# One transposed form of the tokens in the first phase, router logits put together from extra matmul columns, and a gathered copy of each sequence's columns

## The chip, the cores and the metric

The kernel runs on one core of one Trainium2 chip. The core has five engines that work side by side, each through its own instructions in program order: TensorE (PE in the profile; its weight loads are shown apart as PEld), VectorE (DVE), ScalarE (ACT), GpSimd (POOL) and SyncE (SP), which here only issues DMAs. An engine that must wait for another one's result stands still, and everything behind the waiting instruction in its own queue stands with it. The metric is the device time of one execution in microseconds (us). Three runs of the kernel before took 988.33, 989.93 and 993.07 us; the median is 989.93 us.

## What is computed

The input is 32 "rows" s of 256 positions b with 128 features. It is normalised, and the result xn goes into two blocks; the output is x plus both.

```python
xn = _layernorm(x, axis=-1)
x = x + _L0_attn_ref(xn, ...) + _L0_ffn_ref(xn, ...)
```

The first block (`_L0_attn_ref`) is an attention over the 256 positions of each of the 32 rows, 16 heads of 8 features; its scores are a covariance of q and k plus a product of their variances. In the kernel this is the second phase, and a "sequence" there is one s with its 256 positions.

The second block (`_L0_ffn_ref`) is an ordinary transformer layer whose sequence runs the other way: over the 32 values of s at one position b. It normalises xn again (weights ln1), projects to q, k, v, does causal attention of 32 x 32 with 16 heads, projects out, adds the input (x1), normalises x1 (weights ln2), computes eight router logits, and sends each token to its two best experts:

```python
hn = layernorm(x, ln1_w, ln1_b);  qkv = hn @ in_proj_w.T + in_proj_b
...
x1 = x + attn @ out_proj_w.T + out_proj_b
hn2 = layernorm(x1, ln2_w, ln2_b)
logits = hn2 @ router_w.T
```

In the kernel the attention and the router inputs are the first phase; the routing and the experts run inside the second phase.

## The kernel before

**First phase.** The 8192 tokens are cut into 16 chunks (`NCHUNK`) of 512, four tiles k of 128 tokens; a tile holds four positions c of 32 tokens each. `first_rounds` is a software pipeline of rounds i = -2 to 15. Round i works on several chunks at once: it loads chunk i+5, normalises i+3 (`norms`), measures i+4 (`measure`), transposes i+2 (`turn_in`), projects i+2 to k, q and v (`project_in`), spreads the v of i+1 through DRAM (`spread`), computes the scores of i+1, takes the softmax of i and i+1 in four groups g (`lessened` on DVE, `exponents` on ACT, `turn_weights` on PE and ACT), weighs v for i and i-1 (`weigh`, `divide`), and projects out, adds and measures i-1 (`turn_out`, `project_out`). Behind these come `normalise` of i-1 (GpSimd) and `turn_normed` and `logits` of i-2. The order of the calls in the round is written out by hand, and it is the order in which every engine meets its instructions.

Two transposed forms of the tokens are made there: `turn_in` transposes xn (L305, into `xnT`, kept for the second phase) and the twice normalised tokens zn (L310, into `hT`, with ln1's weight and bias applied on the way out of PSUM). `turn_normed` (L442) makes a third, ln2's result, which is used for the router alone (L448).

**PSUM.** The eight PSUM banks are two pools of four, `bank_u` and `bank_w`. A tile takes the bank of its pool that was released longest ago. So if tiles of one pool are used up in the order in which they are made, a tile takes the bank of the tile made four places before it, and waits until that one has been read for the last time. In one round of before, `bank_u` hands out, in this order: pta, ptb, po (second half), ptp0, ptp1, pto, pq, pv, ptp2, ptp3, ptc, po (first half), pl.

**Second phase.** 32 sequences, two units u each; `step(t)` makes score blocks (`sm` and their transposes `sT`), takes maxima on DVE (L622), exponentials on ACT (L625), and weighs (L634). `project` (L557) multiplies a sequence's transposed tokens, read straight out of `xnT` with a step of 32 elements, by Wq, Wk, Wv. `route` is a generator whose steps are dealt out between the units, four a unit up to t = 96 and eight a unit after; its first 49 steps work out the routing and the next 128 scatter the tokens to DRAM (L801). The experts follow in the middle of the phase. `last_rounds` deals out the end of the first phase between the first seven steps of the second.

Of the kernel before, what the change touches and what calls it, by code (L numbers as in the profile page):

```python
# [68 lines left out]
def block_kernel(  # L69
# [26 lines left out]
    xv = x.rearrange("s (i c k) e -> i c s (k e)", c=4, k=4)  # L96
# [7 lines left out]
    xnT = cp.tile([P, NCHUNK, 512], F32, name="xnT")  # L104
# [14 lines left out]
    rv = resd.rearrange("s (i c k) e -> i c s (k e)", c=4, k=4)  # L119

    vec = cp.tile([P, 7], F32, name="vec")
    l1w, l1b, l2w, l2b = (vec[:, n:n + 1] for n in range(4))
# [5 lines left out]
    mhalf = cp.tile([P, 4, 1], F32, name="mhalf")  # L128
    wqkv = cp.tile([P, 3, P], F32, name="wqkv")
    wo = cp.tile([P, P], F32, name="wo")  # L130
    inT = cp.tile([P, 3, P], F32, name="inT")
    outT = cp.tile([P, P], F32, name="outT")
    rT = cp.tile([P, NE], F32, name="rT")

# [5 lines left out]
    def load(i):  # L140
        xt = ax.tile([P, 4, P], F32, tag="xt", name=f"xt{i}")
        for c in range(4):
            nc.sync.dma_start(xt[32 * c:32 * c + 32].rearrange("s k e -> s (k e)"), xv[i, c])
        return xt
# [13 lines left out]
    late = xnT[:, NCHUNK - 2:NCHUNK].rearrange("p i t -> p (i t)").rearrange("p (n m) -> p n m", m=P)  # L158
    ipw, opw, qkw, rw, bvs = late[:, 0:3], late[:, 3], late[:, 4:6], late[0:NE, 6], late[:, 7]
    qkT, ccen = zx[:, NTILE - 2:NTILE], zx[:, NTILE - 3]  # L160

    def loads():
# [7 lines left out]
        nc.scalar.dma_start(opw, out_proj_w)  # L170
        nc.scalar.dma_start(bout, out_proj_b.partition_broadcast(P))
# [3 lines left out]
        nc.sync.dma_start(rw, router_w)  # L175
# [5 lines left out]
    def set_in():  # L181
        nc.vector.tensor_scalar(bk4, cst[:, C_M4:C_M4 + 4], bk, None, ALU.mult)
        pt = bank_u([P, 4, P], "pt0")
        for n in range(3):
            nc.tensor.transpose(pt[:, n, :], ipw[:, n, :], ident)
        nc.tensor.transpose(pt[:, 3, :], opw, ident)
        nc.vector.tensor_copy(inT[:, 0:2, :], pt[:, 0:2, :])

        nc.vector.tensor_copy(
            inT[:, 2, :].rearrange("p (j g d) -> p j g d", j=4, g=4),  # L190
            pt[:, 2, :].rearrange("p (g j d) -> p j g d", j=4, g=4),
        )
        nc.vector.tensor_copy(outT, pt[:, 3, :])


        nc.vector.tensor_copy(bvs, bv.to_broadcast([P, P]))
        pbo = bank_u([P, P], "pbo")
        nc.tensor.matmul(pbo, bvs, outT, start=True, stop=True)
        nc.vector.tensor_tensor(bout, bout, pbo, ALU.add)

    def set_rest():
        pt = bank_w([P, 4, P], "pt1")
        nc.tensor.transpose(pt[:, 0, :], qkw[:, 0, :], ident)
        nc.tensor.transpose(pt[:, 1, :], qkw[:, 1, :], ident)
        nc.tensor.transpose(pt[:, 2, 0:NE], rw, ident[0:NE, 0:NE])
        nc.vector.tensor_copy(qkT, pt[:, 0:2, :])
        nc.vector.tensor_copy(rT, pt[:, 2, 0:NE])
# [3 lines left out]
        nc.vector.tensor_copy(wqkv[:, 0:2, :], pb)  # L211

# [42 lines left out]
    xts, rss, nrm, mvs, zns, hTs, qTs, kbt, scs, prs, pTs, wps, os, oTs, x1s, h2s = ({} for _ in range(16))  # L255

    def stats(src, tag, i, bufs=2):

        st = a2.tile([P, 4, 6], F32, tag="st", name=f"st{tag}{i}")
        mv = a2.tile([P, 4, 2], F32, tag=f"mv{tag}", name=f"mv{tag}{i}")  # L260
# [3 lines left out]
        rs = a2.tile([P, 4, 1], F32, tag=f"rs{tag}", name=f"rs{tag}{i}")  # L264
# [4 lines left out]
    def measure(i):  # L269
# [10 lines left out]
        nc.gpsimd.tensor_tensor(r2, r2, mhalf, ALU.pow)  # L280
        nrm[i] = rs, nb, r2

# [20 lines left out]
    def turn_in(i):  # L303

        nc.scalar.copy(  # L305
            xnT[:, i, :].rearrange("p (c k s) -> p k c s", c=4, k=4),
            transposed(tokens(i), "a", i).rearrange("p (k c s) -> p k c s", k=4, c=4),
        )
        hTs[i] = a2.tile([P, 512], F32, tag="hT", name=f"hT{i}")
        nc.scalar.activation(hTs[i], transposed(zns.pop(i), "b", i), AF.Identity, bias=l1b, scale=l1w)  # L310
        nc.gpsimd.tensor_tensor(tokens(i), tokens(i), bout.unsqueeze(1).to_broadcast([P, 4, P]), ALU.add)

    def project_in(i):
        hT = hTs.pop(i)
        pk = bank_w([P, 512], f"pk{i}")
        nc.tensor.matmul(pk, inT[:, 1, :], hT, start=True, stop=True)  # L316
# [5 lines left out]
        nc.tensor.matmul(pq, inT[:, 0, :], hT, start=True, stop=True)  # L322
        qTs[i] = a2.tile([P, 512], F32, tag="qT", name=f"qT{i}")
        nc.scalar.activation(qTs[i], pq, AF.Identity, bias=bq, scale=1.0)
        pv = bank_u([P, 4, 4, 32], f"pv{i}")
        for k in range(4):
            nc.tensor.matmul(pv[:, :, k, :], hT[:, k * P:(k + 1) * P], inT[:, 2, :], start=True, stop=True)
        nc.scalar.copy(
            vs[i % 2].rearrange("p j k g d -> p (j k g) d")[:, :, 0:HD],
            pv.rearrange("p j k (g d) -> p (j k g) d", d=HD),  # L330
        )
        nc.sync.dma_start(vald[i], vs[i % 2].rearrange("p j k g d -> p j (k g d)"))
# [86 lines left out]
    def project_out(i):  # L419

        oT = oTs.pop(i)
        px = bank_w([P, 4, P], f"px{i}")
        for k in range(4):
            nc.tensor.matmul(px[:, k, :], oT[:, k * P:(k + 1) * P], outT, start=True, stop=True)  # L424
        x1 = x1s[i] = a2.tile([P, 4, P], F32, tag="x1", name=f"x1{i}")
        nc.vector.tensor_tensor(x1, px, tokens(i), ALU.add)
# [3 lines left out]
        for c in range(4):  # L430
            nc.sync.dma_start(rv[i, c], xt[32 * c:32 * c + 32].rearrange("s k e -> s (k e)"))

    def normalise(i, eng=nc.gpsimd):
        x1, mv, rs = x1s.pop(i), mvs.pop(i), rss.pop(i)
        for k in range(4):
# [4 lines left out]
    def turn_normed(i):  # L440
        h2s[i] = a2.tile([P, 512], F32, tag="h2", name=f"h2{i}")
        nc.scalar.activation(h2s[i], transposed(tokens(i), "c", i), AF.Identity, bias=l2b, scale=l2w)  # L442

    def logits(i):
        pl = bank_u([P, 4, NE], f"pl{i}")
        h2 = h2s.pop(i)
        for k in range(4):
            nc.tensor.matmul(pl[:, k, :], h2[:, k * P:(k + 1) * P], rT, start=True, stop=True)  # L448
        nc.vector.tensor_copy(lg[:, 4 * i:4 * i + 4, :], pl)
# [4 lines left out]
    def first_rounds():  # L454
# [6 lines left out]
        set_in()  # L461
        measure(1)
        set_values(0)
        for i in range(-2, NCHUNK):
# [23 lines left out]
            if i == NCHUNK - 1:  # L488
                project(0, 0)
# [12 lines left out]
            if chunk(i + 3):  # L502
                norms(i + 3)
            if chunk(i + 4):
# [4 lines left out]
            if chunk(i - 1):  # L509
                normalise(i - 1)  # L510
            if chunk(i + 1):
                scores(i + 1)
            if chunk(i - 2):
                turn_normed(i - 2)
# [10 lines left out]
            if chunk(i - 2):  # L525
                logits(i - 2)

    def last_rounds():
# [5 lines left out]
        yield turn_normed(n - 1)  # L534
        yield project_out(n)
        yield logits(n - 1)
        yield normalise(n, nc.vector)
        yield turn_normed(n)
        yield logits(n)
# [5 lines left out]
    xs_all = xnT.rearrange("p i (b s) -> p (i b) s", s=NB)  # L545
    NU = 2 * NB
    pps = {}
    ot, qas, kas, exs, pos, oas, res = {}, {}, {}, {}, {}, {}, {}
# [5 lines left out]
    def project(s, ti):  # L554
# [3 lines left out]
            pp.rearrange("p n m -> p (n m)"), xs_all[:, ti * P:(ti + 1) * P, s],  # L558
# [4 lines left out]
        nc.scalar.activation(sq, pqk, AF.Square, scale=1.0 / math.sqrt(HD - 1))  # L563
        qk = qkts[s % NQ][:, ti].rearrange("p n g m r -> p (n g m) r")
        nc.scalar.copy(qk[:, :, 0:HD], pqk)
        pps[s, ti] = pp, sq

    def project_rest(s, ti):
# [4 lines left out]
        nc.scalar.copy(vo[:, :, 0, 0:8], pi[:, :, 0])  # L573
        qk = qkts[s % NQ][:, ti].rearrange("p n g m r -> p (n g m) r")
        nc.vector.tensor_reduce(qk[:, :, HD:HD + 1], sq, AX.X, ALU.add)
        nc.vector.tensor_copy(vo[:, :, 1, 8:16], pi[:, :, 1])
# [140 lines left out]
    def route():  # L717
# [3 lines left out]
        oh1, oh2 = r_tile("oh1", NTILE, NE), r_tile("oh2", NTILE, NE)  # L721
        yield nc.vector.tensor_reduce(m, lg, AX.X, ALU.max)
# [69 lines left out]
        for name, dram, src, dt in (("posb", posd, posi, I32), ("gateb", gated, gates, F32)):  # L792
            dv = dram.rearrange("s (i c k) u -> c s i (k u)", c=4, k=4)
            for c in range(4):
                nc.sync.dma_start(dv[c], src[32 * c:32 * c + 32].rearrange("p (i k) u -> p i (k u)", k=4))
# [146 lines left out]
    def step(t):  # L942
# [21 lines left out]
        if x == 6 and 0 <= u < NU:  # L964
# [56 lines left out]
```

## Time and profile before

The profile is of one execution that took 992.8 us, of which the span below (first to last instruction) is 991.0 us. Its first phase is the first 260 us or so; the rest is the second phase.

| where | span us | PE busy | DVE busy | ACT busy | POOL busy | granted PE clock |
|---|---|---|---|---|---|---|
| 0 to 25 (start) | 25 | 11.05 | 7.50 | 10.37 | 14.12 | 1.00 |
| 50 to 75 | 25 | 22.79 | 17.98 | 20.59 | 16.95 | 1.00 |
| 175 to 200 | 25 | 22.76 | 16.90 | 19.92 | 17.86 | 0.93 |
| 250 to 275 | 25 | 21.19 | 15.34 | 10.28 | 11.26 | 0.93 |
| 275 to 300 | 25 | 22.27 | 22.48 | 11.00 | 2.50 | 0.86 |
| 600 to 800 | 200 | 200.00 | 120.59 | 126.23 | 106.20 | 1.00 |

PE busy counts matmuls from start to modelled end, and as they are pipelined they overlap: it says whether PE had work, not how well the array was used. The granted clock is the share of full speed that PE was given.

The projection to k (`pk`, L316) happens once a round, so its starts are a clock for the rounds. They are at 15.91, 28.12, 40.90, 53.54, 67.45, 82.23, 99.47, 115.86, 131.48, 145.32, 159.56, 173.45, 189.56, 203.39, 219.54 and 232.69 us.

### The profile page before, as it was taken

The numbers are of one execution on the slowest core, as the hardware profiler recorded it, in microseconds if no ns is written. First come the engines' busy times: TensorE is split into PE (matmuls) and PEld (weight loads), VectorE is DVE, ScalarE is ACT, GpSimd is POOL, SyncE is SP. The second block draws the span as 40 slices with busy tenths as digits, with TensorE's granted clock in tenths as the row PEclk, the third lists the DMA queues.
The fourth block names the chain that finished last, engine by engine and source line by source line (L and its number), as shares of the span: only waits on it lengthen the run. The fifth ranks groups of instructions, "written<-read, shape, count | busy, mean of one in ns | idle before, by whom it ended". The sixth has DMA issues, their size and how long they took to land.

```text
span 991.0 us, 32300 instructions
## 1 busy us (share of the span) xinstructions
PE 940.2 (95%) x13107; PEld 679.0 (69%) x13107; DVE 706.3 (71%) x1638; ACT 655.1 (66%) x1362; POOL 561.9 (57%) x725
## 2 busy tenths in 40 slices
PE   4788999989789999999999999999999999999998
PEld 2567777777666666666666689999866666666664
DVE  2477578667589999888888834444588888888882
ACT  4687878877446666666666665555666666676664
POOL 5468787785310002777777123333387888888870
PEclk9798999999889999999999999999999999999999
DMA  3344434422031000541111134444222321121220
GB/s 100 108 132 125 134 120 139 140 60 68 21 102 35 2 2 15 59 111 55 55 53 54 52 117 135 133 134 136 76 60 63 81 69 36 39 68 52 55 60 22
DMA packets 87747, 76.32 MB, mean 77 GB/s; under 512 B 32840, under 2 KB 70864, under 8 KB 87600
## 3 DMA queue, kind: packets, MB, share of 16 engines
q1 hardware_dynamic: 74736, 48.03, 17.4%
q0 software_dynamic: 11600, 26.10, 8.5%
q8 instruction: 103, 1.69, 0.7%
q10 hardware_dynamic: 1264, 0.14, 0.1%
q14 instruction: 44, 0.36, 0.1%
HBM read 33.98 MB, written 40.24 MB: 75 GB/s over the span
## 4 chain that ended last, share of the span: by engine, by line
PE 86%; DVE 7%; issue 2%; POOL 2%; ACT 1%; DMA 0%; ACTq 0%; DVEq 0%; SPq 0%; POOLq 0%
PE sm L610 26%; PE pav L634 13%; PE pe L854 6%; PE pp L557 6%; PE ph L845 6%; PE pqk L584 3%; PE ptp L300 2%; PE sT L616 2%; PE pt L653 2%; PE sc L359 2%; DVE pr L375 2%; PE px L834 2%; PE pk L316 2%; PE px L424 2%; PE py L687 2%
## 5 line engine op out<-in xcount | busy, mean ns | idle before, releaser
L625 ACT ACTIVATE ex<-sT 128x512 f32<-128x512 f32 x512 | 277.7, 595 | 179.0 <-PE sT L616 179.0
L622 DVE TENSOR_REDUCE mt<-sm 128x2 f32<-128x512 f32 x512 | 329.0, 686 | 73.6 <-PE sT L616 67.7
L610 PE MATMUL sm<-ka,qa 32*128 32x256 f32 x2048 | 292.4, 402 | 3.5 <-DVE mt L622 3.5
L616 PE MATMUL sT<-qa,ka 32*128 32x256 f32 x2048 | 291.0, 400 | 0.0
L610 PEld LDWEIGHTS sm<-ka,qa 32*128 32x128 f32 x2048 | 177.4, 185 | 81.0 <-issue 38.1
L616 PEld LDWEIGHTS sT<-qa,ka 32*128 32x128 f32 x2048 | 176.4, 184 | 2.6 <-issue 1.7
L801 POOL DMA_INDIRECT xsd<-zx,posi x128 | 122.9, 960 | 81.4 <-DVE posi L789 42.7
L905 POOL DMA_INDIRECT yg<-ysd,posb x128 | 122.1, 954 | 43.0 <-issue 31.5
L634 PE MATMUL pav<-ex,va 128*32 128x256 f32 x2048 | 137.2, 385 | 0.0
L859 POOL DMA_DIRECT2D ysd<-ye x71 | 48.2, 679 | 115.0 <-DVE ye L858 89.1
L634 PEld LDWEIGHTS pav<-ex,va 128*32 128x32 f32 x2048 | 53.8, 109 | 64.2 <-issue 24.0
L854 PEld LDWEIGHTS pe<-w,ge 128*128 128x128 f32 x568 | 74.5, 192 | 4.2 <-ACT ge L847 0.7
L854 PE MATMUL pe<-w,ge 128*128 128x128 f32 x568 | 74.9, 275 | 0.3 <-ACT ge L847 0.3
L845 PE MATMUL ph<-xT,w 128*128 128x256 f32 x284 | 73.3, 381 | 0.0
L557 PE MATMUL pp<-wqkv,xnT 128*128 128x384 f32 x128 | 65.6, 595 | 0.8 <-DVE mt L622 0.8
L858 DVE COPY ye<-pe 128x256 f32<-128x256 f32 x71 | 30.1, 424 | 50.8 <-PE pe L854 50.8
L837 ACT ACTIVATE xT<-px,vec 128x256 f32<-128x256 f32 x71 | 39.9, 563 | 35.8 <-PE px L834 35.8
L847 ACT ACTIVATE ge<-ph 128x512 f32<-128x512 f32 x71 | 42.4, 597 | 21.1 <-PE ph L845 21.1
L378 ACT ACTIVATE pr<-pr 128x1024 f32<-128x1024 f32 x32 | 33.8, 1058 | 34.0 <-DVE pr L375 33.9
L374 DVE TENSOR_REDUCE mx<-sc 128x16 f32<-128x512 f32 x64 | 43.4, 678 | 17.3 <-PE sc L359 17.3
L828 DVE COPY w<-wall 128x512 f32 x71 | 30.4, 429 | 33.3 <-issue 31.9
L845 PEld LDWEIGHTS ph<-xT,w 128*128 128x128 f32 x284 | 48.5, 191 | 4.1 <-ACT xT L837 0.4
(170 smaller groups left out, 1663.0 us busy)
## 6 DMA issues: line engine op xcount, KB each, us to landing
xb<-xsd SPq DMA_DIRECT2D x71, 128.0 KB, 2.1
ysd<-ye POOLq DMA_DIRECT2D x71, 128.0 KB
xsd<-zero SPq DMA_DIRECT2D x10, 852.0 KB
vald<-v SPq DMA_DIRECT2D x16, 288.0 KB, 2.3
vb<-vald SPq DMA_DIRECT2D x64, 72.0 KB, 3.0
xt<-in_L_attn_x_dram SPq DMA_DIRECT2D x64, 64.0 KB, 2.0
resd<-xt SPq DMA_DIRECT2D x64, 64.0 KB, 1.7
res<-resd SPq DMA_DIRECT2D x32, 128.0 KB, 3.3
```

What stands on the lines that cost most here:

```text
L374: nc.vector.tensor_reduce(mx, s, AX.X, ALU.max)
L557: nc.tensor.matmul(pp.rearrange("p n m -> p (n m)"), xs_all[:, ti * P:(ti + 1) * P, s], wqkv.rearrange("p n m -> p (n m)"), start=True, st ...
L610: nc.tensor.matmul(sc[:, i, :], qas[u][r:r + 32, i * P:(i + 1) * P], kas[u][r:r + 32, h, :], start=True, stop=True,)
L616: nc.tensor.matmul(sc[:, i, :], kas[u][r:r + 32, h, i * P:(i + 1) * P], qas[u][r:r + 32, :], start=True, stop=True,)
L622: nc.vector.tensor_reduce(mts[y // 8 % 2][:, :, o:o + 1], sc, AX.X, ALU.max, negate=True)
L625: nc.scalar.activation(exs[y], sc, AF.Exp, scale=1.0 / HD)
L634: nc.tensor.matmul(pos[u][32 * j:32 * j + 32, :], vaugs[s % NV][:, ti, 4 * j + 2 * g + h, :], exs[8 * u + 4 * h + j][:, ti, :], start=(h = ...
L801: yield nc.gpsimd.indirect_dma_start(xsd_views[n * NTILE + k], bass.IndirectOffsetOnAxis(ap=posi[:, k, n:n + 1], axis=0), zx[:, k, :], None,)
L845: nc.tensor.matmul(ph[:, f, :], wb[n][0][:, f * P:(f + 1) * P], xT, start=True, stop=True)
L854: nc.tensor.matmul(pe[:, j, :], ge[:, f, j * P:(j + 1) * P], w2b[:, f, :], start=(f == 0), stop=(f == 1))
L859: nc.gpsimd.dma_start(ysd[n * BLK:(n + 1) * BLK].rearrange("(p j) h -> p j h", j=2), ye)
L905: yield nc.gpsimd.indirect_dma_start(yg[s][:, ti, n, :], None, ysd, bass.IndirectOffsetOnAxis(ap=gt["posb"][:, s, ti, n:n + 1], axis=0),)
```

## The change

The first phase keeps one transposed form. `turn_in` transposes only zn, and a plain copy keeps it as `znT` for both phases. ln1's weight is multiplied into the projection weights and its bias into the projection biases (`set_in`). The second phase needs xn and not zn: xn is zn divided by a factor r2 per token, so `invert` keeps 1/r2 (`rall`) on DVE, `scale_back` transposes it, sends it to DRAM and reads it back by sequence (`rpos`), and `project`, `project_rest` multiply by it while they copy out of PSUM. `gather` copies a sequence's 256 columns out of `znT` to a contiguous tile, on ACT, ahead of `project`.

The logits no longer come from a transposed ln2 result. Eight more columns of the v projection (`inV`, 160 instead of 128) give the part that comes from zn, scaled by `rall` on DVE; eight more columns of the out projection (`outX`, 136 instead of 128) give the part from the attention. `set_rest` works out three constant rows, and five GpSimd steps at the head of `route` apply mean, scale and offset. `turn_normed` and `logits` are gone. The wider results don't fit one PSUM bank, so `pv` and `px` are two tiles each. Half of `normalise` (tiles 2 and 3) moves from GpSimd to DVE, and to the end of the round. Tokens are ordered (k, c) instead of (c, k) in a chunk, so that token loads, residual stores and the posd/gated stores have shorter contiguous pieces (512 bytes for 2 KB, 8 bytes for 32).

```diff
-    xv = x.rearrange("s (i c k) e -> i c s (k e)", c=4, k=4)
+    xv = x.rearrange("s (i k c) e -> i c s k e", c=4, k=4)
...
+    inT = cp.tile([P, 2, P], F32, name="inT")
+    inV = cp.tile([P, 5, 32], F32, name="inV")
+    outX = cp.tile([P, P + NE], F32, name="outX")
...
+    def invert(i):
+        nc.vector.reciprocal(rall[:, 4 * i:4 * i + 4], r2s.pop(i).rearrange("p k o -> p (k o)"))
...
     def turn_in(i):
-        nc.scalar.copy(
-            xnT[:, i, :].rearrange("p (c k s) -> p k c s", c=4, k=4),
-            transposed(tokens(i), "a", i).rearrange("p (k c s) -> p k c s", k=4, c=4),
-        )
-        hTs[i] = a2.tile([P, 512], F32, tag="hT", name=f"hT{i}")
-        nc.scalar.activation(hTs[i], transposed(zns.pop(i), "b", i), AF.Identity, bias=l1b, scale=l1w)
+        nc.scalar.copy(znT[:, i, :], transposed(zns.pop(i), "b", i))
...
     def project_in(i):
...
-        pv = bank_u([P, 4, 4, 32], f"pv{i}")
-        for k in range(4):
-            nc.tensor.matmul(pv[:, :, k, :], hT[:, k * P:(k + 1) * P], inT[:, 2, :], start=True, stop=True)
+        for h in range(2):
+            pv = bank_u([P, 5, 2, 32], f"pv{i}_{h}")
+            for k in range(2):
+                o = (2 * h + k) * P
+                nc.tensor.matmul(pv[:, :, k, :], zT[:, o:o + P], inV, start=True, stop=True)
+            nc.scalar.copy(
...
+            nc.vector.tensor_tensor(
+                lg[:, t, :], pv[:, 4, :, 0:NE], rall[:, t].unsqueeze(2).to_broadcast([P, 2, NE]), ALU.mult
+            )
...
     def project_out(i):
...
+        for h in range(2):
+            px = bank_w([P, 2, P + NE], f"px{i}_{h}")
+            for k in range(2):
+                o = (2 * h + k) * P
+                nc.tensor.matmul(px[:, k, :], oT[:, o:o + P], outX, start=True, stop=True)
+            nc.vector.tensor_tensor(
+                x1[:, 2 * h:2 * h + 2, :], px[:, :, 0:P], tokens(i)[:, 2 * h:2 * h + 2, :], ALU.add
+            )
+            l = lg[:, 4 * i + 2 * h:4 * i + 2 * h + 2, :]
+            nc.vector.tensor_tensor(l, l, px[:, :, P:P + NE], ALU.add)
...
+    def scale_back():
+        pr = bank_u([NTILE, P], "pra")
+        nc.tensor.transpose(pr, rall, ident)
+        ra = a1.tile([NTILE, P], F32, tag="ra", name="ra")
+        nc.vector.tensor_copy(ra, pr)
+        nc.sync.dma_start(rnd.rearrange("(n c) s -> n (c s)", c=4), ra)
+        nc.sync.dma_start(rpos[:, 0], rnd.rearrange("(i t) s -> t i s", t=P))
+        nc.vector.tensor_scalar(rpos[:, 1], rpos[:, 0], 1.0 / math.sqrt(HD - 1), None, ALU.mult)
...
             if i == NCHUNK - 1:
+                gather(0)
+                gather(1)
                 project(0, 0)
...
+            if chunk(i + 3):
+                invert(i + 3)
...
-                normalise(i - 1)
+                normalise(i - 1, nc.gpsimd, (0, 1))
             if chunk(i + 1):
                 scores(i + 1)
-            if chunk(i - 2):
-                turn_normed(i - 2)
...
             if chunk(i):
                 divide(i, 0)
-            if chunk(i - 2):
-                logits(i - 2)
+            if chunk(i - 1):
+                normalise(i - 1, nc.vector, (2, 3))
+            if i == NCHUNK - 3:
+                scale_back()
...
+    def gather(s):
+        xs[s] = bh.tile([P, SEQ], F32, tag="xs", name=f"xs{s}", bufs=2)
+        nc.scalar.copy(xs[s], xs_all[:, :, s])
...
-            pp.rearrange("p n m -> p (n m)"), xs_all[:, ti * P:(ti + 1) * P, s],
+            pp.rearrange("p n m -> p (n m)"), xs[s][:, ti * P:(ti + 1) * P],
...
-        nc.scalar.activation(sq, pqk, AF.Square, scale=1.0 / math.sqrt(HD - 1))
+        nc.scalar.activation(sq, pqk, AF.Square, scale=rpos[:, 1, ti, s:s + 1])
...
-        nc.scalar.copy(qk[:, :, 0:HD], pqk)
+        nc.scalar.activation(qk[:, :, 0:HD], pqk, AF.Identity, scale=rpos[:, 0, ti, s:s + 1])
...
+        yield nc.gpsimd.tensor_tensor(
+            t, mvall[:, :, 0:1].to_broadcast(all8), rows[:, 1:2, :].to_broadcast(all8), ALU.mult
+        )
+        yield nc.gpsimd.tensor_tensor(lg, lg, t, ALU.subtract)
+        yield nc.gpsimd.tensor_tensor(lg, lg, rows[:, 0:1, :].to_broadcast(all8), ALU.add)
+        yield nc.gpsimd.tensor_tensor(lg, lg, rsall.to_broadcast(all8), ALU.mult)
+        yield nc.gpsimd.tensor_tensor(lg, lg, rows[:, 2:3, :].to_broadcast(all8), ALU.add)
```

## Prediction

> **What bounds the kernel now.** I read the busy time by stretches first. Columns: stretch and length, then busy us of PE, PEld, DVE, ACT, POOL with instruction counts, PE's granted clock, DMA share, GB/s.
>
> ```profile
> 150.00:175.00 25.00, 23.20 (x617) 17.68 (x615) 20.18 (x59) 20.35 (x36) 19.72 (x32) 1.00 0.41 124
> 185.00:186.00 1.00, 1.00 (x8) 1.00 (x8) 0.82 (x3) 0.39 (x2) 0.75 (x5) 0.61 0.04 10
> 186.00:187.00 1.00, 1.00 (x25) 0.67 (x27) 0.69 (x1) 0.73 (x2) 0.92 (x2) 0.50 0.30 76
> 187.00:188.00 1.00, 1.00 (x61) 0.92 (x51) 0.06 (x1) 0.57 (x1) 1.00 (x2) 0.50 0.04 6
> 188.00:189.00 1.00, 1.00 (x7) 1.00 (x7) 0.96 (x3) 0.12 (x1) 1.00 (x3) 0.68 0.21 64
> 350.00:500.00 150.00, 150.00 (x1900) 96.64 (x1896) 129.44 (x281) 101.42 (x241) 84.55 (x88) 1.00 0.22 51
> ```
>
> The second phase is PE alone: 150 of 150 us. The first phase isn't: no engine is full, and four are at 80 to 93%. That is the mark of a loop that passes from engine to engine. To find it I read one undisturbed round in the timeline (start, length, engine, line, operation, count, idle before it).
>
> ```profile
> 160.53 1.06 ACT L378 ACTIVATE pr<-pr 128x1024 f32<-128x1024 f32 x1 [0.57 <-DVE pr L375]
> 161.50 0.57 ACT L417 COPY oT<-pto 128x512 f32<-128x512 f32 x1
> 161.96 2.79 ACT L320 ACTIVATE kb<-pk,bk,cst 128x512 f32<-128x512 f32 x4
> 162.12 0.97 PEld L424 LDWEIGHTS px<-outT,oT 128*128 128x128 f32 x8
> 163.38 0.69 DVE L426 TENSOR_TENSOR x<-px,zx 128x512 f32<-128x512 f32 x1 [2.94 <-PE px L424]
> 164.62 0.71 ACT L324 ACTIVATE qT<-pq,vec 128x512 f32<-128x512 f32 x1
> 167.40 0.66 DVE L374 TENSOR_REDUCE mx<-sc 128x16 f32<-128x512 f32 x1
> 172.69 0.42 DVE L413 TENSOR_TENSOR o<-po,aden 128x256 f32<-128x256 f32 x1
> 173.75 0.69 DVE L375 TENSOR_TENSOR pr<-sc,mx 128x512 f32<-128x512 f32 x1
> ```
>
> DVE idles once, 2.94 us before L426. From there to 174.44 it is never idle. Then ACT's L378 and L417 follow (1.06 + 0.57), then px, then L426 again: 14 us. A second ring has the same length: from the end of oT (162.07), ACT copies kb and qT (to 165.33), PE makes the scores (L359, 1.83 us in the chain of waits), DVE takes their maxima at 167.40, runs to 174.44, and ACT closes it with L378 and L417 at about 176.1: 14.0 us. Rounds without a clock dip take 13.2 to 14.2, mean 13.8, by the starts of pk; the last twelve average (232.69 - 53.54)/12 = 14.93, the rest being dips and some early waits for GpSimd.
>
> **The change, part by part.** *PE in the first phase.* Lengths are from the chain of waits. Removed per round: pta 0.49, ptc 0.59, pl 0.99, together 2.07. Added: pv's eight passes take 0.89 for 128 columns, so 160 columns take 1.11 (+0.22), and px's 136 columns +0.06. PE loses 1.8 us a round. None of it lies between qT and the maxima, nor between L413 and px: they fill PE while DVE works, so removal by itself shortens neither ring.
>
> *ACT.* Removed: L305 0.57, L442 0.81; L310 falls from 0.78 to about 0.57 (as L305); v in two halves adds about 0.2. Gone are 1.4 us that lie in ACT's waits for DVE. Worth nothing on the rings.
>
> *DVE.* Two tiles of normalise at 0.33 each (L436's four DVE instances), 0.27 apart: +0.6. They stand between `divide(i, 0)` and the next `lessened`, inside both rings. The lg copy (0.18, 0.1 apart) goes. x1 in halves with two small additions is 2 x (0.42 + 0.17) for 0.69, about +0.55; invert +0.16; the lg products wait for pv and finish while px runs. These 0.7 us stand between px and the statistics, so they load the first ring only.
>
> *A PSUM wait that is new.* bank_u's order in a round becomes ptb, po, ptp0, ptp1, pto, pq, pv0, pv1, ptp2, ptp3, po. Four back from ptp3 was pto, read by L417 before px; now it is pq, read by qT (L324), which ACT reaches only after four kb copies, 3.3 us after px's start. PE is in order, so behind ptp3 stand the four causal matmuls (L347) and all scores. Before, these were done when qT came; now ptp3 (four transposes, 0.44 as pto) and L347 (four, 0.86 at the spacing of 0.21) come after it: scores +1.3 us later. On the second ring, not hidden. The first ring's +0.7 fits into this: statistics end 5.5 us after oT, scores 6.6.
>
> Round: 13.8 + 1.3 + 0.6 - 0.1 = **15.6 us** without dips.
>
> *Clock dips, a rule against a row.* The Trainium skill's page "TensorE: Matmul & The Clock Gate" (section "What's actually happening") says that PE falls to half clock after an idle window of about 3.4 us. The rows above show 0.50 for about 3 us, and ahead of them stands a much shorter gap:
>
> ```profile
> 183.80 0.36 PE L395 MATMUL po<-vb,pT 128*32 128x36 f32 x18 [1.65 <-issue]
> ```
>
> There are six such dips between 93 and 254 us, four of about 3 us and two longer; one of 3 us costs half of it, 1.6. By the rule, the new gaps (some 1.8 us before qT, 2 us before ptp0, 1.4 us before the last pto) cause no dip, and the round stays at 15.6; by the row they cause more of them than before, up to 1.7 a round. As a dip now falls partly into PE's slack, I take +0.5.
>
> Sum over rounds: 12 x (15.6 + 0.5 - 14.93) = +14; two earlier rounds (12.7 each, not yet full) about +1 each.
>
> *scale_back.* Its last DVE instruction waits for a DRAM write and the read of it. No such pair is in the trace; nearest are xt 2.0 or vald 2.3 us to land, then xb 2.1 or vb 3.0: 4.1 to 5.3, plus transpose and copy. Behind it in DVE's queue stands `lessened(14, 2)`, on the ring. Bounds 0 (slack after all) and 6; I take +5, as with vald and vb.
>
> *Rounds 14, 15 and start.* No pq there, but normalise and the halves: +2.5 for both. At the start, set_in's DVE list grows by about 2 us (two small copies, a 384-element product and sum) ahead of pbo, less pta and a shorter copy: +1 (0.3 to 2.5, the larger if 512-byte loads land later; vb's 576-byte pieces take 3.0 us for xt's 2.0). ACT's queue issues two more loads (l1bs, and rw from SP's queue) at 0.45 each; it ends issuing at 4.7 us and first computes at 9.15. From round 15 on, two gathers +1, turn_normed and logits gone -1.5.
>
> *Second phase.* The weight load of pp:
>
> ```profile
> L557 PEld LDWEIGHTS pp<-wqkv,xnT 128*128 128x128 f32 x128 | 33.0, 305 | 21.7 <-issue 17.2 <-DVE mt L622 3.2 <-DVE cnt L736 0.7
> L845 PEld LDWEIGHTS ph<-xT,w 128*128 128x128 f32 x284 | 48.5, 191 | 4.1 <-ACT xT L837 0.4
> ```
>
> Same shape, 305 ns against 191, and only L557 reads with a step. The first of pp's two loads stands open (pp takes 0.95 in the chain for 0.64 of streaming), so the contiguous copy saves 0.11 x some 55 projections that PE bounds: **-6**. It costs ACT 32 gathers of 0.38 (L589) to 0.61. The larger end adds L557's excess of 0.9 ns per column; the skill's "SBUF — State Buffer" (in section "Door 1: The DMA port swizzle": reads come in 16-byte lines, so that a step of 4 fp32 is free) gives the reason why a step of 32 should cost ACT too, which no row here shows. I take 0.6: 20 us. Scales read per partition add 3 x 64 x 0.11 (L591 493 ns, L589 379): 21 us. ACT idles 179 us waiting for L616, which covers both; without that cover it would be +41. DVE gains 64 x 0.1 on 129 of 150: hidden behind PE.
>
> *Route.* Five POOL steps at 1.28 (L311's size) while POOL is idle from 274 us on; DVE's first reduction of route waits for the last of them, but is dealt out four steps later, when POOL is done. Everything after starts five steps later, and the scatter ends about 4 us after 549.3 (eight steps a unit of 8.7 us). The experts' first transpose is at 569.8, so nothing. The posd and gated stores, four times as many pieces, stand on SP at 396 to 414 us, with 139 us to the next expert fetch (553).
>
> Sum: 14 + 2 + 5 + 2.5 + 1 - 0.5 - 6 = **+18**, so 992.8 becomes 1010.8; the median of the runs shown lies 2.9 lower: **1008 us**.
>
> **Rivals.** *No bank wait (DVE alone).* If ptp3 doesn't wait for qT, the first ring counts: 13.8 + 0.55 + 0.16 + 0.6 - 0.1 + 0.22 - 0.48 (px's first half comes earlier) = 14.75, with 0.3 of dips +1.5 over twelve rounds; with the other terms about +4, **994 us**. For: ring one is real in the rows. Against: the banks' order.
>
> *Dips in every round.* PE idles some 4 us of 16; at 1.7 a round unhidden the round is 17.3: 12 x 2.37 = 28, in all about +32, **1022 us**. For: gaps of 1.65 us sufficed. Against: slack before ptp3.
>
> *PE decides, faster.* PE is at 93% and the chain shows stretches of 14 us of PE alone. If DVE's 2.94 us of idle takes up its additions, rounds follow PE's loss to about 13.1, dips return to 0.5: -16, with scale_back, start and second phase -19 in all: **971 us**. It decides from the point at which DVE has work it may do before px. Against: DVE is in order, and only the lg products stand there.
>
> That logits or scales are not computed as said, I see no sign of.
>
> **Numbers.** Forecast 1008 (own range 999 to 1018): 0.50. No bank wait 0.17, dips 0.15, PE decides 0.16, else 0.02. A difference under 0.5% (5 us) can't be told from none. Slower: forecast and dips whole, half of "no bank wait", 0.74; same 0.07; faster 0.19. Range 980 to 1030: it leaves out most of the faster case and a tail above.
>
> **What would show it.** pk's starts 15.5 to 16.5 apart; ptp idle until ACT qT, and DVE's mx waiting for PE sc each round (before: mostly not); DVE idle about 5 us for a DMA of rpos near the end of the phase; pp's load near 190 ns; the second phase 6 us shorter. Wrong if rounds stay under 14.5, if ptp3 never waits for ACT, or if the second phase isn't PE's alone.

## The result, and the profile after

The changed kernel takes 1086.88 us (median of 4 runs, 1085.74 to 1088.25), the kernel before 991.5 us in the same session: ratio 1.0966, interval 1.093 to 1.1002. The forecast of 1008 us had the sign, was 79 us short, and its range (980 to 1030) doesn't hold the result. The profiled execution has a span of 1086.5 us against 991.0, so 95.5 us have to be found.

Two clocks show where. The first is the start of `pk`, once a round (L351 now). The second is the start of `pp`, once a unit (L611 now, L557 before). Differences are after less before:

| up to | difference, us | added there, us |
|---|---|---|
| first `pk` | 0.8 | 0.8 |
| last `pk`, 15 rounds later | 31.9 | 31.1 |
| first `pp` | 43.6 | 11.7 |
| 17th `pp` | 48.0 | 4.4 |
| 21st `pp` | 55.1 | 7.1 |
| 22nd `pp` | 95.1 | 40.0 |
| 64th and last `pp` | 93.7 | -1.4 |
| end of the span | 95.5 | 1.8 |

Busy time by stretches in the changed kernel (columns as in the prediction) shows two troubles of different kinds.

```profile
150.00:175.00 25.00, 19.18 (x484) 14.05 (x482) 16.13 (x62) 15.92 (x31) 12.03 (x19) 0.93 0.36 112
350.00:440.00 90.00, 89.99 (x1086) 56.09 (x1085) 85.19 (x182) 64.36 (x146) 1.52 (x6) 1.00 0.01 2
440.00:500.00 60.00, 49.30 (x554) 30.09 (x552) 38.55 (x80) 33.81 (x76) 32.83 (x34) 0.91 0.90 37
500.00:525.00 25.00, 0.00 (x0) 0.00 (x0) 0.00 (x0) 0.00 (x0) 11.49 (x12) 0.50 0.76 40
```

In the first row every engine is less busy than before in the same stretch (DVE 16.13 for 20.18, although it has more to do): the loop waits more. In the last, PE, DVE and ACT do nothing for 25 us, and at 40 GB/s the DMA engines are busy 0.76 of the time. The row before has a DMA share of 0.90 at 37 GB/s.

**The round.** This is one round in the timeline (start, length, engine, line, operation, count, idle before it).

```profile
182.52 0.57 ACT L460 COPY oT<-pto 128x512 f32<-128x512 f32 x1
182.98 2.79 ACT L355 ACTIVATE kb<-pk,bk,cst 128x512 f32<-128x512 f32 x4
185.64 0.70 ACT L359 ACTIVATE qT<-pq,vec 128x512 f32<-128x512 f32 x1
186.21 0.67 ACT L367 COPY v<-pv 128x256 f32<-128x256 f32 x2
186.40 0.42 PEld L341 LDWEIGHTS ptp<-cst,pr 128*128 128x128 f32 x4 [1.84 <-ACT qT L359]
186.64 0.45 DVE L372 TENSOR_TENSOR lg<-pv,rall 128x16 f32<-128x16 f32 x2 [5.18 <-ACT v L367]
187.00 0.41 DVE L471 TENSOR_TENSOR x<-px,zx 128x256 f32<-128x256 f32 x1
191.12 0.66 DVE L417 TENSOR_REDUCE mx<-sc 128x16 f32<-128x512 f32 x1
```

The wait that the forecast named is there: ptp's fourth group, 1.84 us behind `qT`. But another is longer. DVE stands 5.18 us at its small product for `lg`, until ACT has copied `v` out of the same PSUM tile. From 90 to 265 us this happens in ten rounds and takes 52.3 us of DVE in all. ACT reaches that copy only after four kb copies and `qT`. DVE is in order, so `x`, both statistics and the maxima follow. When the maxima come at 191.12 they wait for nobody: the scores are ready, so ptp's wait lies beside this one. The last twelve rounds take 17.22 us on average (14.93 before, 16.1 forecast).

**The stall.** These are SP's transfers around it (start, then the time over which SP issues them), first three of the five steps of the kernel before, then all five of the changed one. The residual fetches are the last.

```profile
396.45 2.71 SPq L795 DMA_DIRECT2D posd<-posi  x4
402.63 3.23 SPq L798 DMA_DIRECT2D posb<-posd  x2
418.00 8.89 SPq L552 DMA_DIRECT2D res<-resd  x10
```

```profile
448.75 15.51 SPq L858 DMA_DIRECT2D posd<-posi  x4
480.52 3.24 SPq L861 DMA_DIRECT2D posb<-posd  x2
483.81 15.74 SPq L858 DMA_DIRECT2D gated<-gates  x4
518.45 3.81 SPq L861 DMA_DIRECT2D gateb<-gated  x2
522.32 8.46 SPq L606 DMA_DIRECT2D res<-resd  x10
```

And this is the instruction of DVE that PE's chain hangs on, from the timeline.

```profile
528.61 0.42 DVE L743 TENSOR_TENSOR res<-res,py 128x256 f32<-128x256 f32 x1 [39.14 <-DMA res<-resd]
```

Before, the four steps ahead of the residual fetch held SP from 396.45 to 418.00; now it is from 448.75 to 522.32. SP can begin to read `posd` back only when its stores have landed: 31.8 us after the first store's issue (480.52 - 448.75), 6.2 before. DVE begins to wait for the residual at 489.5 (528.61 - 39.14). For 32.9 us of its 39.14 the fetch isn't even issued; once issued, it lands after 6.2 us. So it is the place in SP's queue that makes it late. ACT and PE wait behind DVE.

**scale_back and pp.** A timeline line, and a line of the costliest groups:

```profile
283.54 0.20 DVE L497 TENSOR_SCALAR rpos<-rpos 128x64 f32<-128x64 f32 x1 [5.26 <-DMA rpos<-rnd]
```

```profile
L611 PEld LDWEIGHTS pp<-wqkv,xs 128*128 128x128 f32 x128 | 19.5, 192 | 26.8 <-issue 17.9 <-DVE mt L677 5.0 <-ACT xs L602 3.3
```

DVE stands 5.26 us for the scales' way through DRAM (forecast 5), and pp's weight load takes 192 ns for 305 (forecast near 190). `gather` takes ACT 637 ns a sequence (forecast 0.6 us).

Some of the runs below fell on other chips, on which every kernel, the one before too, loses about 240 us while GpSimd scatters and gathers (1229 to 1247 us for the kernel before); for the argument only the stretch of these runs ahead of the scatter is used, up to the 17th `pp`.

### The profile page after: what moved, and what is told of

Read it like the earlier page. It is cut to its first block, busy times and chain, and to the rows that moved or that the text cites. A ratio compares the mean times of both kernels' runs of the same rounds, so it can differ in the third digit from the quotient of the medians.

```text
span 1086.5 us, 31870 instructions
## 1 busy us (share of the span) xinstructions
PE 932.0 (86%) x12861; PEld 651.4 (60%) x12861; DVE 731.4 (67%) x1759; ACT 668.5 (62%) x1378; POOL 545.6 (50%) x700
## 4 chain that ended last, share of the span: by engine, by line
PE 64%; DVE 14%; DMA 7%; ACT 6%; issue 3%; POOL 2%; SPq 2%; DVEq 0%; ACTq 0%; POOLq 0%
PE sm L665 22%; PE pav L689 11%; PE pe L917 6%; PE ph L908 5%; PE pp L611 4%; DVE pr L418 3%; ACT kb L355 3%; DVE mx L417 3%; DMA posd<-posi 2%; PE pqk L639 2%; DMA gated<-gates 2%; PE sT L671 2%; PE pt L708 2%; PE px L897 1%; SPq L858 1%
## 5 line engine op out<-in xcount | busy, mean ns | idle before, releaser
L665 PE MATMUL sm<-ka,qa 32*128 32x256 f32 x2048 | 302.0, 407 | 42.8 <-DVE va L631 39.0
L671 PE MATMUL sT<-qa,ka 32*128 32x256 f32 x2048 | 296.5, 405 | 1.4 <-ACT ex L680 1.4
L665 PEld LDWEIGHTS sm<-ka,qa 32*128 32x128 f32 x2048 | 184.4, 187 | 123.9 <-issue 66.0
L671 PEld LDWEIGHTS sT<-qa,ka 32*128 32x128 f32 x2048 | 179.6, 187 | 4.6 <-ACT ex L680 2.0
L689 PE MATMUL pav<-ex,va 128*32 128x256 f32 x2048 | 139.6, 390 | 0.0
L301 POOL TENSOR_SCALAR rsall<-mvall 128x4 f32<-128x4 f32 x16 | 3.7, 232 | 127.7 <-DVE rall L322 80.5
L341 PE MATMUL ptp<-cst,pr 128*128 128x128 f32 x256 | 45.4, 323 | 23.2 <-ACT qT L359 15.7
L611 PE MATMUL pp<-wqkv,xs 128*128 128x384 f32 x128 | 59.7, 549 | 5.6 <-ACT xs L602 3.0
L372 DVE TENSOR_TENSOR lg<-pv,rall 128x16 f32<-128x16 f32 x32 | 5.6, 175 | 86.4 <-ACT v L367 84.8
```

Of the source, the lines that this page charges most:

```text
L341: nc.tensor.transpose(pt[:, k, :], src[:, k, :], ident)
L611: nc.tensor.matmul(pp.rearrange("p n m -> p (n m)"), xs[s][:, ti * P:(ti + 1) * P], wqkv.rearrange("p n m -> p (n m)"), start=True, stop=True,
L665: nc.tensor.matmul(sc[:, i, :], qas[u][r:r + 32, i * P:(i + 1) * P], kas[u][r:r + 32, h, :], start=True, stop=True,)
L671: nc.tensor.matmul(sc[:, i, :], kas[u][r:r + 32, h, i * P:(i + 1) * P], qas[u][r:r + 32, :], start=True, stop=True,)
L689: nc.tensor.matmul(pos[u][32 * j:32 * j + 32, :], vaugs[s % NV][:, ti, 4 * j + 2 * g + h, :], exs[8 * u + 4 * h + j][:, ti, :], start=(h = ...
```

## The experiments

**e1_rows: the stores in rows.**

```diff
-    posd = dp.tile([NB, SEQ, 2], I32, name="posd")
+    posd = dp.tile([P, NTILE, 2], I32, name="posd")
...
-            dv = dram.rearrange("s (n c) u -> c s n u", c=4)
-            for c in range(4):
-                nc.sync.dma_start(dv[c], src[32 * c:32 * c + 32])
+            nc.sync.dma_start(dram, src)
...
-                nc.sync.dma_start(dst[:, :, ti, :], dram[:, ti * P:(ti + 1) * P, :].rearrange("s t u -> t s u"))
+                nc.sync.dma_start(dst[:, :, ti, :], dram[:, 32 * ti:32 * ti + 32].rearrange("(c s) m u -> m c s u", c=4))
```

> posd and gated keep a tile's layout in DRAM, so that each is stored in one transfer of 512-byte rows instead of four of 8-byte pieces; the reads back gather the same 8-byte pieces as before. Store theory (the 8-byte stores hold SP's queue, and the residual fetch that PE's second-phase chain needs stands behind them): the 39-us wait of DVE at L743 for the residual goes nearly whole, about 1048 us (1043 to 1055). Rival, route itself is late (its new POOL steps and the scatter push the residuals or the exponentials back): the wait shrinks by 10 us at most, above 1075 us.

Measured: 1037.51 us, ratio 1.0476 (1.0413 to 1.0538), 49.4 us below the changed kernel. The first, second and fifth step of SP's queue:

```profile
446.43 0.34 SPq L856 DMA_DIRECT2D posd<-posi  x1
448.02 4.10 SPq L859 DMA_DIRECT2D posb<-posd  x2
460.44 7.29 SPq L606 DMA_DIRECT2D res<-resd  x10
```

The four steps take 14 us for 73.6, the residual is fetched at 460, and PE is busy for 39.3 of the 40 us from 440 to 480. From the 17th to the 22nd `pp` only 1.0 us is added to the distance from before (45.7 to 46.7), where the changed kernel adds 47.1, so the 7 us ahead of the big stall belonged to the stores too. The rival falls.

**b1_order: the new order of tokens alone, in the kernel before.**

```diff
-    xv = x.rearrange("s (i c k) e -> i c s (k e)", c=4, k=4)
+    xv = x.rearrange("s (i k c) e -> i c s k e", c=4, k=4)
...
-            dv = dram.rearrange("s (i c k) u -> c s i (k u)", c=4, k=4)
+            dv = dram.rearrange("s (n c) u -> c s n u", c=4)
```

> The kernel before with one part of the change alone: the new order of tokens (x and the residual in 512-byte pieces, xnT copied straight, posd and gated stored in 8-byte pieces). Store theory: the stall of the changed kernel appears whole, 991 + 36 to 40, about 1029 us (1022 to 1034), with DVE's wait for the residual near 35 us. Rival (the stall needs the later start of the second phase or the new route steps): 988 to 998 us.

Measured: 1023.25 us, ratio 1.0308 (1.0248 to 1.0367). Up to the 17th `pp` this execution is 3.6 us ahead of the kernel before. That isn't shown to be the order's gain: b3c below has the same order and is 4.3 us behind there. From the 17th `pp` to the 22nd the stores take 36 us. The stall needs neither the later phase nor the new route. Busy time by stretches shows what fills the DMA engines:

```profile
390.00:450.00 60.00, 47.16 (x545) 29.44 (x540) 34.01 (x72) 30.27 (x71) 32.65 (x35) 0.89 1.03 42
```

The last two columns are the DMA share, 1.03, and the rate, 42 GB/s; the kernel before has 0.42 and 81 GB/s in the same stretch. The engines are full, and move less.

**e1b_res_act: the residual fetch on ACT's queue.**

```diff
-        nc.sync.dma_start(res[s], resd[s].rearrange("(i t) e -> t i e", t=P))
+        nc.scalar.dma_start(res[s], resd[s].rearrange("(i t) e -> t i e", t=P))
```

> The residual fetch is issued from ACT's queue instead of SP's; the 8-byte stores stay. Queue theory (only the place behind the stores on SP makes the residual late): the 39-us wait goes, about 1048 us (1044 to 1056), with some 0.5 us an issue on ACT hidden behind PE. Rival, the DMA engines (the pieces of the stores fill the engines, so that a fetch from any queue lands late): 10 us of wait or more remain, above 1058 us.

Measured: 1237.49 us, so neither. ACT's waits tell why:

```profile
ACT ex L680 <- DMA xb<-xsd: 86.7, 1, 86.7
ACT ex L680 <- DMA out_dram<-res: 62.8, 5, 32.3
```

Ahead of such an exponential stands a residual fetch in ACT's queue (at 624.36 us, with the exponential at 624.88 after 86.67 us of waiting). The fetch carries waits that SP could stand through and ACT can't. So the time prices a waiting transfer on a busy engine's queue. The trace still answers a part of what the run was made for: two fetches were issued on ACT's queue while the stores of `gated` were under way (478.57 to 510.76), at 479.83 and 501.25 us, and landed after 6.3 and 10.3 us (median of that trace 2.0). Full DMA engines make a fetch slower by 4 to 8 us here, not by 39.

**e5_ahead: the fetches ahead of the stores, still on SP.**

```diff
+    EARLY = {0: [*range(6)], **{n: [n + 5] for n in range(1, 11)}, **{n: [] for n in range(11, 16)}}
...
-                for s in RESIDUALS.get(u // 2, [u // 2] if u // 2 < NB - 6 else []):
+                for s in EARLY.get(u // 2, RESIDUALS.get(u // 2, [u // 2] if u // 2 < NB - 6 else [])):
```

> The changed kernel with nothing but the residual fetches of sequences 1 to 15 issued five sequences earlier on SP's queue, so that those which PE's chain needs stand ahead of the stores; the 8-byte stores stay as they are. Queue theory (the residual is late only because its fetch stands behind the stores): the 39-us wait goes nearly whole, about 1047 us (1043 to 1052), a little above e1_rows for the 5-us wait near the first store. Rival, the pieces themselves fill the DMA engines: 1055 us or more.

It ran on one of the other chips: 1272.72 us for 1230.25, ratio 1.0343. No instruction waits for a residual any more, but the starved stretch hides what that is worth. The reading that the queue's order makes the residual late therefore rests on the moments of issue and landing in the changed kernel and in e1b_res_act, not on a time of this run.

**e2_lg_first: DVE reads pv ahead of ACT.**

```diff
...
+            nc.vector.tensor_tensor(
+                lg[:, t, :], pv[:, 4, :, 0:NE], rall[:, t].unsqueeze(2).to_broadcast([P, 2, NE]), ALU.mult
+            )
             nc.scalar.copy(
                 v[:, :, 2 * h:2 * h + 2].rearrange("p j k g d -> p j (k g) d")[:, :, :, 0:HD],
...
-            nc.vector.tensor_tensor(
-                lg[:, t, :], pv[:, 4, :, 0:NE], rall[:, t].unsqueeze(2).to_broadcast([P, 2, NE]), ALU.mult
-            )
```

> In project_in DVE's product for lg is put ahead of ACT's copy of v in the program, so that ACT waits for DVE at the bank of pv and not DVE for ACT. Theory of the lg wait (DVE, in order, stands at L372 behind ACT's four kb copies, qT and v, and x, the statistics and the maxima behind it): rounds fall from 17.2 to about 16.1, where the wait of ptp's fourth group for qT takes over, so 10 to 18 us less, about 1073 us. Rival, the bank wait of ptp already sets the round and the lg wait only lies beside it: under 4 us less, above 1083 us. Third: ACT now waits for a DVE that is itself late, no gain or a loss.

Measured: 1058.49 us, ratio 1.0682 (1.0621 to 1.0743): 28.4 us less, more than expected. The rounds are now the forecast's: 15.6 us, nine of the last twelve to a tenth. At the first `pp` 20.4 us are gained; the other 8 come up to the 22nd, most of them from a smaller stall (35.3 us at the 22nd `pp` for 40.0).

**e12c: both.** Two earlier executions of it, e12 and e12r, fell on the other chips: 1270.12 us for 1246.86, and 1262.66 for 1228.74.

> The row-shaped stores of posd and gated and the lg product ahead of the copy of v, together. If the two losses are separate, their gains add: 1086.9 - 49.4 - 28.4 = 1009 us (1004 to 1014), the size of the forecast on record. If they share part of a wait (the residual is late by a time of day, not by a span), less: 1014 to 1024 us.

> e12 a third time. On a chip on which the scatter leaves the second phase alone: 1020 us (1014 to 1024) by its start of the 17th projection in the two runs so far; if the two gains add whole, 1009 us. Where the scatter takes PE's instructions away again, only the stretch up to the 17th projection counts: 29 us behind the kernel before.

Measured (e12c): 1020.83 us, ratio 1.0298 (1.0272 to 1.0324). The two share 12 us of their gains (49.4 + 28.4 = 77.8; together 66.1). Most of that, 8.3 us, is what e2 gained behind the first `pp`: it lay in the stall, which e1 takes away in any case. One round of it in the timeline:

```profile
186.03 0.17 DVE L368 TENSOR_TENSOR lg<-pv,rall 128x16 f32<-128x16 f32 x1 [1.47 <-PE pv L366]
186.08 2.79 ACT L355 ACTIVATE kb<-pk,bk,cst 128x512 f32<-128x512 f32 x4
187.04 0.42 DVE L471 TENSOR_TENSOR x<-px,zx 128x256 f32<-128x256 f32 x1 [0.29 <-PE px L470]
188.74 0.70 ACT L359 ACTIVATE qT<-pq,vec 128x512 f32<-128x512 f32 x1
189.50 0.42 PEld L341 LDWEIGHTS ptp<-cst,pr 128*128 128x128 f32 x4 [1.84 <-ACT qT L359]
192.69 0.69 DVE L417 TENSOR_REDUCE mx<-sc 128x16 f32<-128x512 f32 x1 [1.40 <-PE sc L402]
```

`lg` is done while ACT is at kb, `x` starts 1.4 us after `oT`, not 4.5, and the maxima now wait 1.40 us for the scores. They come 3.25 us after the end of `qT` (188.74 + 0.70 to 192.69), 2.07 in the kernel before (165.33 to 167.40): 1.2 us later, and the forecast had 1.3.

**e123 and e124: one more edit each, on e12.** e123 makes `qT` ahead of kb:

```diff
+        pq = bank_u([P, 512], f"pq{i}")
+        nc.tensor.matmul(pq, inT[:, 0, :], zT, start=True, stop=True)
+        qTs[i] = a2.tile([P, 512], F32, tag="qT", name=f"qT{i}")
+        nc.scalar.activation(qTs[i], pq, AF.Identity, bias=bq, scale=1.0)
         for j in range(4):
             m = cst[:, C_M4 + j:C_M4 + j + 1]
             nc.scalar.activation(kb[:, j, :], pk, AF.Identity, bias=bk4[:, j:j + 1], scale=m)
...
```

> As e12, and ACT makes qT ahead of the four kb copies. Theory of the bank wait (ptp's fourth group, 0.65 us, and the causal matmuls, 0.86 us, stand behind qT's read of pq on the ring of 15.6 us): they now run beside the kb copies, the rounds fall to about 14.1 us, 12 x 1.5 = 18 us less than e12, about 991 us (986 to 996). Rival, another ring is close behind (px, the statistics, the maxima): under 6 us less than e12.

e124 moves the instruction that waits for the DMA (`e4_scale_late` does that alone, on the changed kernel):

```diff
-        nc.vector.tensor_scalar(rpos[:, 1], rpos[:, 0], 1.0 / math.sqrt(HD - 1), None, ALU.mult)
...
             if i == NCHUNK - 1:
+                nc.vector.tensor_scalar(rpos[:, 1], rpos[:, 0], 1.0 / math.sqrt(HD - 1), None, ALU.mult)
                 gather(0)
```

> As e12, and the scaling of rpos[:, 1] is issued on DVE in the last round ahead of the gathers, not behind the DMA in round 13. Theory of scale_back (DVE stands 5.3 us for the read back on the ring, and PE's clock falls for a while after): 5 to 8 us less than e12, about 1003 us. Rival, the wait has slack or comes back at the handover: under 2 us less.

> The changed kernel with DVE's scaling of rpos[:, 1] moved from behind the DMA in round 13 to the last round. Theory of scale_back (5.26 us of DVE on the ring): 5 to 8 us less, 1079 to 1082 us. Rival (the next bound of those rounds takes its place): under 3 us less.

e123 and e124 took 1267.18 and 1265.62 us for 1246.86, e4_scale_late 1266.62 for 1230.25, all on the other chips. So I read the 17th `pp`, behind the kernel before: e12 29.4 us, e123 23.2, e124 25.1. By this `qT` first is worth 6.2 us, not 18, and scale_back's move 4.3, a little less than expected. Alone on the changed kernel, the move takes 48.0 to 42.3: 5.7 us. These are single executions: other runs that have the changed kernel's program up to there stand between 45.7 (e1_rows) and 48.0 (e5_ahead), so 5.7 can be as little as 3.4.

In e123 rounds of 14.5 do occur, 1.1 us under those of e12, but four in twelve are over 15.5. Three of these lie between 98 and 150 us, where PE waits for GpSimd's `zn` ahead of ptb, up to 3.5 us at a time. From 60 to 260 us these waits come to 15.5 us in e123, 8.6 in e12 and 3.1 in the kernel before. So a part of what the bank wait gives is taken by the next one; how much isn't measured, as no run here removes it.

**e1234c and e1234n: all four, then normalise back on GpSimd.** Two earlier executions of e1234c, e1234 and e1234r, fell on the other chips: 1259.63 us for 1246.86, and 1249.14 for 1228.74.

```diff
-                normalise(i - 1, nc.gpsimd, (0, 1))
+                normalise(i - 1, nc.gpsimd, range(4))
...
-            if chunk(i - 1):
-                normalise(i - 1, nc.vector, (2, 3))
```

> All four edits. If they are independent: e12 - 18 - 6 = about 985 us (979 to 992), below the kernel before by little. If the ring of DVE is then the bound, 3 to 8 us above that.

> e1234 a third time: 1008 us (1003 to 1012) on such a chip; on the other kind, 17 to 18 us behind the kernel before at the 17th projection.

> As e1234, with all four tiles of normalise back on GpSimd as before. Theory (0.51 us of DVE's normalise stand on the ring in each round): rounds of 14.5 fall to 14.0, 7 to 8 us less than e1234, about 1000 us, or 10 us behind the kernel before at the 17th projection. Rival, GpSimd is too full for it (62% busy, and ptb waits for its zn): no gain, or a loss of up to 10 us.

The first expectation, 985 us, was too good by the 12 us that `qT` didn't give and the 12 us that the first two edits share. Measured: e1234c 1011.58 us, ratio 1.0182 (1.0147 to 1.0218); e1234n 1004.62 us, ratio 1.014 (1.0112 to 1.0167). So DVE's two tiles are worth some 7 us by the medians and 7.6 at the 17th `pp`, and GpSimd has room for them. The last twelve rounds average 15.65 us in e12c, 15.13 in e1234c, 14.88 in e1234n and 14.93 in the kernel before. In e1234c, too, PE waits for GpSimd from 60 to 260 us, 15.4 us in all and 4.9 in e12c:

```profile
PEld ptb L341 <- POOL zn L336: 15.4, 8, 3.5
```

The granted clock over the same stretch is lower as well, 0.91 for 0.98 (0.92 before). But e12, the same program as e12c, has 0.93 with rounds of 15.70, so what the clock takes isn't shown.

What remains of e1234n over the kernel before is 11.3 us at the 17th `pp`: 5.1 up to the last `pk` (start 1.2, first three rounds 4.4, later ones -0.5), 2.5 from there to the first `pp`, 3.7 after it.

**b2_rows and b3: the good parts alone.** b3 is the kernel before with the new order, stores in rows, and the gather; b2 is the same without the gather.

```diff
-            pp.rearrange("p n m -> p (n m)"), xs_all[:, ti * P:(ti + 1) * P, s],
+            pp.rearrange("p n m -> p (n m)"), xs[s][:, ti * P:(ti + 1) * P],
```

> The kernel before with the new order of tokens and the stores of posd and gated in 512-byte rows. b1_order was 3.6 us ahead of the kernel before up to the stall, which goes here: about 987 us (984 to 990). Rival, the order is worth nothing by itself: 990 to 993 us.

> b3_gather again (the kernel before, the new order of tokens, stores in rows, gathered columns). By its first run, 4.8 us ahead of the kernel before at the 16th projection, and another 3 us over the rest of the second phase: 982 to 986 us, faster than both kernels.

b2 and b3's first run fell on one of the other chips (1229.25 and 1228.29 us for 1228.74). b3c: 988.91 us for 991.26, ratio 0.9975 (0.9957 to 0.9992), 3 us above what was expected. It is 98 us faster than the changed kernel; its distance to the kernel before is less than the 0.5% that I said can be told from none. From the 10th `pp` (4.8 us behind before in the profiled execution) to the last (0.3 ahead) it gains 5.1 us, and the gathers cost nothing that shows. That this is the contiguous weight load fits b1_order, which has the order without the gather: from the 22nd `pp` to the last it goes from 32.3 to 33.9 us behind, b3c from 3.8 behind to 0.3 ahead.

## Where the prediction failed, and what of it was right

**The rounds: one clause failed.** "The lg products wait for pv and finish while px runs." They wait for ACT, too. Both instructions only read `pv`, from the same tile and so from the same bank, and DVE's stands second in the program. Swapping the two removes the wait behind ACT, so two readers of one tile are enough for it; whether the tile or its bank counts isn't separated here. The forecast put this wait at nothing; it takes 5.18 us of DVE in the round shown, and e2 puts it at 28.4 us of the kernel. With the swap the other steps of the round hold: 1.84 us of ptp behind `qT`, the maxima 1.2 us later (1.3 forecast), 0.60 for two tiles of normalise (0.6), rounds of 15.6. The kernel before had a row for it. In this piece of its timeline both engines read `pqk`, at the start of the second phase:

```profile
287.68 0.48 ACT L591 ACTIVATE ka<-pqk,cst 128x256 f32<-128x256 f32 x1
288.19 0.48 DVE L592 TENSOR_SCALAR ka<-pqk,cst 128x256 f32<-128x256 f32 x1 [1.21 <-ACT ka L591]
```

DVE starts as ACT ends (287.68 + 0.48 = 288.16) after waiting 1.21 us. These two also write one tile, so the row alone doesn't say which sharing counts; it should have raised the question.

**The stores: the wrong successor.** "The posd and gated stores, four times as many pieces, stand on SP at 396 to 414 us, with 139 us to the next expert fetch (553)." The pieces were counted, but their landing was taken from the old ones, and the next thing on SP's queue is not an expert fetch: it is ten residual fetches at 418, of which PE's chain needs one every 17.4 us. Price: 49.4 us by e1, 0 in the forecast.

**What is left.** Without these two losses e12c is 26.6 us behind the kernel before in its trace, where the sum had 18. That is nearer by errors that cancel in part: 13.7 us up to the last `pk`, where the start and the rounds had 17; 10.7 from there to the first `pp`, where scale_back and the rest had 7; and +2.1 from the first `pp` to the last, where the second phase had -6.

**Dips: rule against row.** The round without dips was 15.6 in the sum, 16.1 with 0.5 for dips. With the lg wait gone, the rounds are 15.65, and the clock 0.98 although PE stands 1.84 us in each. So here the sum by the rule of the Trainium skill (page "TensorE: Matmul & The Clock Gate", section "What's actually happening") was nearer than the row of 1.65 us. But neither foretells the dips of these kernels. The kernel before has six dips between 93 and 254 us, and from 60 to 260 no gap of its matmuls is longer than 2.16 us, where the rule speaks of about 3.4. And two executions of one program, with like waits, have a clock of 0.98 (e12c) and 0.93 (e12) from 60 to 260 us.

**The terms beside them.** scale_back: +5 forecast, 5.26 of wait, 4.3 by e124 and up to 5.7 by e4_scale_late; right. The start: +1, measured 0.8; right. The handover from the last `pk` to the first `pp`: 2.5 - 0.5 besides scale_back, measured 11.7 less 5.7, so 6: the sum was too low by 4, and where these lie wasn't tried. Second phase: -6 forecast; the load does give 0.07 to 0.09 us a unit (47.0 us behind at the 18th `pp`, 43.7 at the last, in e1_rows; 5.1 over 54 units in b3c), but 3.3 to 4.6 us are lost over the first 17 units in every version that keeps the scales and the longer route. b3c, which has gathers and neither of these, stays at 3.9 to 4.8 there. Which of the two it is wasn't tried.

**The rivals.** "No bank wait" and "PE decides" fall with e12c's lines. "Dips in every round" had the size of the rounds nearest (17.3 for 17.22) by luck: the cause was another. Two of their sums don't come out as listed: the terms of "no bank wait" give +5.5 and not about +4, those of "PE decides" -16 and not -19; nothing rests on it. None held a DVE that waits for ACT at a bank; so even with the stores mended (1037.5 us) the kernel lies outside the range.

## What to carry to other kernels

When an edit gives a PSUM tile a second reader on another engine, count it as a wait in program order, find what stands ahead of the first reader on its engine, and put the reader with the short queue first. When transfers are cut into smaller pieces, list everything that is issued behind them on the same queue, to the first that a bound engine needs, and take their landing from a row with pieces of that size that go the same way, to or from DRAM. Mending five places brought back 82 of 95 us and still left no gain: in e1234n the rounds are as long as before (14.88 for 14.93 us), although PE has an estimated 1.8 us less to do in each. A part removed from an engine that isn't on the ring pays for nothing that is added on it.

## What was unexpected of the hardware

**Stores in 8-byte pieces are dear, reads of them are not.** This is the ordinary DMA queue in three stretches: the changed kernel from 448 to 480.5 us (posd stored in 8-byte pieces), from 480.5 to 484 (posd read back in 8-byte pieces), and the kernel before from 396 to 402.6 (posd stored in 32-byte pieces).

```profile
q1 hardware_dynamic: 8256, 0.07, 53.7%
q1 hardware_dynamic: 3411, 0.03, 52.8%
q1 hardware_dynamic: 2112, 0.07, 15.1%
```

The columns are packets, MB and the share of the 16 engines' time. Worked out from these, a packet takes 34 ns of engine time when 8 bytes are stored (0.537 x 32.5 x 16 / 8256), 9 when 8 bytes are read, 8 when 32 bytes are stored. So the number of pieces alone doesn't set the price: e1_rows still reads 8-byte pieces, at 9 ns a packet (0.493 x 10 x 16 / 8501, from 448 to 458 us). GpSimd's scatter runs beside the stores and waits for its own transfers, up to 8.6 us at a time. Whether 8-byte stores are dear alone or only beside such a scatter, no run here separates.

**A scatter that starves the engines on some chips.** On the other chips the second phase nearly stops while GpSimd scatters; e12's busy time in the middle of it (from 400 to 420 us PE is busy all the time):

```profile
480.00:500.00 20.00, 4.10 (x7) 1.21 (x7) 0.00 (x0) 0.00 (x0) 15.13 (x17) 0.50 0.15 51
```

PE issues 7 matmuls in 20 us at a DMA share of 0.15. The busier of its two instruction queues by share moved one packet from 430 to 590 us there, and 17 in e12c, the same program on a chip of the other kind. That the instructions come late because of the scatter fits this, but no run here isolates it.
